# One elementwise product of a graph network's edge layer: VectorE or GpSimd

## The chip, the core and the metric

The kernel runs on one core of a Trainium2 chip. The core has five engines with queues of their own: TensorE (PE, matmul; its weight loads are listed as PEld), VectorE (DVE, elementwise), ScalarE (ACT, functions), GpSimd (POOL) and SyncE (SP, which issues transfers). The transfers themselves run on 16 DMA engines. The metric is the device time of one launch in microseconds (us). Thirteen runs of the kernel before have a median of 5436.42 us and lie between 5418.4 and 5446.99 us.

## The reference

Four graph layers follow each other on 6250 nodes with 128 features and 100000 edges, sorted by their target node. Each layer takes `h = relu(layernorm(x))` and adds its result to `x`. The first averages the neighbours' rows and multiplies by two weight matrices; the third does three such layers; the fourth does three attention layers. The second is the one that matters here, the **product layer**: each edge makes a filter from its weight, and the message that it sends is a product of three vectors and a number, and a node multiplies the messages that arrive.

```python
bf = exp(coeff * (dist[:, None] - centers[None, :]) ** 2)
bf = ssp(bf @ W1 + b1)
bf = ssp(bf @ W2 + b2)
cut = where(dist < R_MAX, 0.5 * (cos(pi * dist / R_MAX) + 1.0), 0.0)
msg = h[src] * edge_feat * bf * cut[:, None]
agg = segment_prod(msg, dst, num_segments=n_nodes)
out = ssp(agg @ W3 + b3)
```

`ssp` is softplus less ln 2, `dist` is the edge weight, `edge_feat` the edge attributes of 128 features.

## The kernel before

The layers run one after the other. In the product layer (`filter_in_order`, from line 846) the edges lie in 128 rows of 784 consecutive edges: partition p holds the edges 784 p to 784 p + 783, the last partition fewer. A column is one edge of each partition. The layer walks the columns in 196 steps of four (`HB`), and its buffers hold eight columns (`NB`). What a step does is spread over six turns of one loop, so that each engine works on another step at the same time; `Pace` and `chain` keep the order in which the loop writes the instructions, on GpSimd for what is handed to `order`, and on PE, DVE and ACT for everything.

For a step i the work is, in this order:

- `inputs(i)`, one turn ahead, in the loop's turn i-1 (line 972): SP loads the edge attributes `ea` (line 883, for eight columns at every second step, in two transfers or three), and GpSimd issues **four gathers** (line 887, recorded at line 67), each of which fetches 128 rows of the node table by the source indices, into four of the eight columns of the tile `rows`. `clocked` (line 888) lets each gather wait for the PE instruction that was written last, the end of `basis` of the same turn. `rows` and `ea` have four buffers each.
- `basis(i)`, turn i: ACT makes the Gaussians `bf` for eight columns at every second step (Square and Exp), and PE makes `z1` with a bias matmul (line 901) and the one with `w1` (line 902).
- `logs(i+2)`, turn i+2: ACT makes the part of the softplus of `z1` that is not linear (Abs, Exp, Ln). The same Exp and Ln serve `z2` of an older step.
- `hidden(i)`, turn i+2: DVE finishes the softplus (`s1`, line 919, shown as s), and PE makes `z2` from a bias (line 921) and four matmuls (line 923).
- **`given(i)`, turn i+3**: the product of the edge attributes with the gathered rows, in place in `ea`, four columns of 128 features at once (line 932, recorded at line 112).
- `factors(i)`, turn i+4: DVE finishes the second softplus (`f2`, line 938, shown as f) and multiplies it by `ea` (line 940).
- `products(i)`, turn i+5: for each column DVE makes `run` (line 957), the running product where the target node is the same as that of the edge before and one where it is not, and multiplies it on (line 959). SP writes the running products `acc` to memory (line 963).

In a turn, `factors(i-4)` and with it the product with `ea` come before `given(i-3)`, so what `given` makes is read one turn later. DVE takes the instructions of `products` between its other ones.

Of the kernel before, what the change touches and what calls it, by code (L numbers as in the profile page):

```python
# [16 lines left out]
OP = mybir.AluOpType  # L17
# [34 lines left out]
def kernel(ctx: ExitStack, tc: tile.TileContext, a: dict, out: bass.AP):  # L52
    nc = tc.nc
# [57 lines left out]
    def tt(o, x, y, op):  # L111
        nc.vector.tensor_tensor(o, x, y, op)  # L112
# [733 lines left out]
    def filter_in_order(table, hist, fl, pool, ps):  # L846
# [9 lines left out]
        order = Pace(0)  # L856
# [69 lines left out]
        def used(i):  # L926
            return 128 if i * HB < L1 else 127

        def given(i):
            h0, n = i * HB % NB, used(i)  # L930
            rows, ea = (x[:n, h0:h0 + HB, :] for x in st["rows", i // 2])
            tt(ea, ea, rows, OP.mult)

        def factors(i, soft):
            h0, n = i * HB % NB, used(i)
# [31 lines left out]
        for i in range(steps + 5):  # L967
            run = products(i - 5) if i >= 5 else iter(())
            if i < steps:
                basis(i)  # L970
            if i < steps - 1:
                inputs(i + 1)
            soft = logs(i) if 2 <= i < steps + 4 else None
            next(run, None)
            if 2 <= i < steps + 2:
                hidden(i - 2, soft)
            next(run, None)
            if 4 <= i < steps + 4:
                for _ in factors(i - 4, soft):
                    next(run, None)  # L980
            next(run, None)
            if 3 <= i < steps + 3:
                given(i - 3)
            for _ in run:
                pass
# [2138 lines left out]
```

## Time and profile before

| what | value |
| --- | --- |
| median of 13 runs | 5436.42 us |
| the profiled execution's own time | 5437.01 us |
| its span, first to last instruction | 5435.2 us |
| busy over the span: PE, DVE, ACT, POOL | 82%, 72%, 61%, 53% |
| gathers of the product layer: count, busy | 784, 804.9 us |
| `ea` times `rows` on DVE: count, median of one | 196, 682 ns |

A group in the profile is a set of instructions of one line, engine, operation and pair of tiles. Its row gives the shapes (partitions x elements), the count, the busy time in us, the mean duration of one in ns, and then the idle time of the engine just before such instructions, with what ended it: "issue" means that nothing in the profile did, "remote" that a semaphore was moved by something that the profile does not tell. An answer for a window counts only what lies in it, in us from the start of the span. The time of a stage is read from its own window, since the shares over the whole span mix layers that are bound by different engines.

### The profile page before, as it was taken

The numbers are of one execution on the slowest core, as the hardware profiler recorded it, in microseconds if no ns is written. First come the engines' busy times: TensorE is split into PE (matmuls) and PEld (weight loads), VectorE is DVE, ScalarE is ACT, GpSimd is POOL, SyncE is SP. The second block draws the span as 40 slices with busy tenths as digits, with TensorE's granted clock in tenths as the row PEclk, the third lists the DMA queues.
The fourth block names the chain that finished last, engine by engine and source line by source line (L and its number), as shares of the span: only waits on it lengthen the run. The fifth ranks groups of instructions, "written<-read, shape, count | busy, mean of one in ns | idle before, by whom it ended". The sixth has DMA issues, their size and how long they took to land. (4 is left out here: it accounts for less than half of the span.)

```text
span 5435.2 us, 83586 instructions
## 1 busy us (share of the span) xinstructions
PE 4478.2 (82%) x25786; PEld 3202.8 (59%) x25786; DVE 3906.1 (72%) x11582; ACT 3315.6 (61%) x6455; POOL 2883.3 (53%) x2871
## 2 busy tenths in 40 slices
PE   1599977787787588899999788889888899788888
PEld 0245533333343255555555677878777788677787
DVE  7998858888888745767687567664666774766664
ACT  5466757777777664433455556667666666656565
POOL 1463047777777536556364366662466662566651
PEclk9999976666656689999999899999999999999999
DMA  4243255555566467888888445443444543444443
GB/s 102 93 170 122 92 173 180 185 184 178 178 185 182 132 181 239 263 252 267 246 268 260 156 128 138 128 132 101 128 129 129 138 134 105 128 126 128 129 128 86
DMA packets 577912, 869.97 MB, mean 160 GB/s; under 512 B 206810, under 2 KB 451991, under 8 KB 569008
## 3 DMA queue, kind: packets, MB, share of 16 engines
q1 hardware_dynamic: 482961, 674.07, 39.7%
q0 software_dynamic: 92160, 188.53, 13.4%
q8 instruction: 205, 3.36, 0.2%
q10 hardware_dynamic: 2332, 1.93, 0.1%
q14 instruction: 254, 2.08, 0.1%
HBM read 565.66 MB, written 298.45 MB: 159 GB/s over the span
## 5 line engine op out<-in xcount | busy, mean ns | idle before, releaser
L67 POOL DMA_INDIRECT rows<-gtable,l_src x1200 | 1195.4, 996 | 795.2 <-issue 291.1
L2604 PE MATMUL cnt<-hot_n,hot_c 128*125 128x250 f32 x3840 | 989.6, 402 | 109.3 <-issue 64.6
L2431 PE MATMUL o<-m,hst 125*128 125x160 f32 x6000 | 954.9, 307 | 102.1 <-issue 99.0
L67 POOL DMA_INDIRECT rows<-table,f_src x784 | 804.9, 1027 | 366.8 <-issue 206.4
L2431 PEld LDWEIGHTS o<-m,hst 125*128 125x128 f32 x6000 | 906.0, 196 | 151.7 <-issue 126.1
L67 POOL DMA_INDIRECT s_rows<-table,s_src x660 | 664.7, 1007 | 419.1 <-issue 174.6
L2604 PEld LDWEIGHTS cnt<-hot_n,hot_c 128*125 128x125 f32 x3840 | 729.3, 199 | 213.1 <-issue 80.8
L2591 ACT ACTIVATE m<-cnt 125x1000 f32<-125x1000 f32 x480 | 478.1, 996 | 449.3 <-remote 213.5
L2422 ACT ACTIVATE hot_c<-hot,coef_t 128x125 f32<-128x125 fp8e4 x1920 | 700.0, 390 | 0.1
L923 PE MATMUL z<-w,s 128*128 128x128 f32 x1568 | 357.0, 399 | 264.4 <-DVE s L121 167.4
L1653 ACT ACTIVATE as_f<-piece 128x1000 fp32r<-128x1000 fp8e4 x390 | 382.1, 1029 | 308.5 <-DMA piece<-adj 99.3
L923 PEld LDWEIGHTS z<-w,s 128*128 128x128 f32 x1568 | 304.3, 289 | 342.5 <-DVE s L121 202.4
L121 DVE SCALAR_TENSOR_TENSOR acc<-acc,ex,rows 125x130 f32<-125x130 f32 x1197 | 424.4, 355 | 35.9 <-issue 0.3
L1544 PE MATMUL o<-as_f,of_two 128*128 128x500 f32 x1560 | 420.1, 414 | 23.0 <-issue 12.0
L1407 ACT ACTIVATE adj<-cnt 128x1000 fp8e4<-128x1000 f32 x250 | 304.2, 1221 | 194.5 <-PE cnt L1406 160.1
L116 DVE TENSOR_SCALAR hot_n<-l_slot,l_id_t 128x250 f32<-128x250 f32 x960 | 301.4, 359 | 167.4 <-remote 88.1
L2421 ACT ACTIVATE hot_n<-half_n 128x250 f32<-128x250 fp8e4 x960 | 384.0, 400 | 18.7 <-issue 10.3
L868 ACT ACTIVATE soft<-z 128x512 f32<-128x512 f32 x392 | 214.6, 585 | 286.4 <-remote 194.4
L1544 PE MATMUL o<-adj,parts 128*128 128x500 fp8e4 x1500 | 359.0, 378 | 0.9 <-ACT adj L1407 0.9
L902 PE MATMUL z<-bf,w 128*128 128x512 f32 x392 | 351.4, 995 | 9.2 <-DMA w_a<-in_L_gnn_W_agg 9.2
L1544 PEld LDWEIGHTS o<-as_f,of_two 128*128 128x128 f32 x1560 | 297.9, 194 | 98.9 <-issue 18.4
L118 DVE TENSOR_SCALAR run<-acc,f_same,f_fresh 128x128 f32<-128x128 f32 (+1 forms) x783 | 298.6, 381 | 19.7 <-DVE acc L121 5.9
(621 smaller groups left out, 7171.8 us busy)
## 6 DMA issues: line engine op xcount, KB each, us to landing
piece<-adj SPq DMA_DIRECT2D x360, 250.0 KB
late_hist<-acc SPq DMA_DIRECT2D x150, 455.0 KB
dist<-ew_dram SPq DMA_DIRECT2D x48, 1024.0 KB
sum_hist<-s_acc SPq DMA_DIRECT2D x132, 320.0 KB
adj<-adj SPq DMA_DIRECT2D x10, 3125.0 KB
hot<-hot SPq DMA_DIRECT2D x240, 128.0 KB
half_n<-node SPq DMA_DIRECT2D x480, 62.5 KB
ea<-in_edge_attr SPq DMA_DIRECT2D x54, 512.0 KB
```

The source lines that it names most:

```text
L67: return nc.gpsimd.indirect_dma_start(out=dst, out_offset=None, in_=table, in_offset=bass.IndirectOffsetOnAxis(ap=idx, axis=0))
L121: nc.vector.scalar_tensor_tensor(o, x, s, y, op0=op0, op1=op1)
L902: nc.tensor.matmul(z1, lhsT=w1, rhs=st["bf"][:, i % 2 * HB:(i % 2 + 1) * HB, :], start=False, stop=True)
L923: nc.tensor.matmul(z2[:, j, :], lhsT=s1[:, j, :], rhs=w2, start=False, stop=j == HB - 1)
L1407: nc.scalar.activation(adj[:, :, NW * (w - w0):NW * (w - w0 + k)].rearrange("p l (w k) -> p w l k", k=NW), cnt[:, :k, :T * NW].rearrange(" ...
L1544: yield nc.tensor.matmul(o[:, :n], lhsT=parts.columns(l, 1, s)[:, 0, :], rhs=adj(l), start=(l == 0 and s == 0), stop=(l == T - 1 and s == ...
L1653: nc.scalar.activation(made[-1], piece[:, at:at + n], AF.Copy)
L2421: nc.scalar.activation(hot_n[:, w, :], half_n[:, w // 2, :], AF.Copy)
L2422: nc.scalar.activation(hot_c[:, w, :P], lt.hot[:, w0 % WB + w, :P], AF.Copy, scale=coef_t[g][:, w0 + w:w0 + w + 1])
L2431: nc.tensor.matmul(o, lhsT=hst[:, l, :D], rhs=m[:P, l, :], start=(l == 0), stop=(l == T - 1))
L2591: nc.scalar.activation(m[:P, :, :, u * 4:u * 4 + 4].rearrange("p l k q -> p k l q"), cnt[:P, :, :T * NW].rearrange("p w (k l) -> p k l w", ...
L2604: nc.tensor.matmul(cnt[:P, w, :T * NW], lhsT=hot_c[:, w, :P], rhs=hot_n[:, w, :], start=True, stop=True)
```

## The change

The product in `given` is handed to GpSimd. It is one instruction on the same tiles, of the same shape and in place as before. It goes through `order.follow`, so that on GpSimd it stands behind the four gathers that `inputs(i + 1)` wrote earlier in the same turn, and ahead of the four gathers of the next turn.

```diff
@@ -929,7 +929,7 @@
         def given(i):
             h0, n = i * HB % NB, used(i)
             rows, ea = (x[:n, h0:h0 + HB, :] for x in st["rows", i // 2])
-            tt(ea, ea, rows, OP.mult)
+            order.follow(nc.gpsimd.tensor_mul(ea, ea, rows))
 
         def factors(i, soft):
             h0, n = i * HB % NB, used(i)
```

## Prediction

> **What bounds the kernel now.** The layers follow each other, so the product layer is a stretch of its own, and what it gains or loses goes into the total. Its bounds come from the first and the last of its gathers (725.4 and 1853.0 us). First view: busy time of the engines in that window. Columns: window, its length, busy us and count of PE, PEld, DVE, ACT, POOL, then granted clock, DMA share and GB/s.
>
> ```profile
> 725.37:1853.03 1127.66, 866.62 (x2334) 426.10 (x2334) 960.72 (x2295) 828.13 (x975) 804.87 (x784) 0.64 0.57 181
> ```
>
> DVE looks like the bound, with 85% (960.72 of 1127.66), and POOL with 71% looks free. That reading would promise a gain. The second view, the groups of 760 to 1850 us, corrects it: look at the idle time behind the bar.
>
> ```profile
> L67 POOL DMA_INDIRECT rows<-table,f_src x758 | 778.8, 1027 | 315.2 <-issue 198.7 <-remote 53.0 <-PE z L902 37.3
> L121 DVE SCALAR_TENSOR_TENSOR s<-z,soft 128x512 f32<-128x512 f32 x190 | 130.2, 685 | 113.5 <-ACT soft L868 97.6 <-issue 13.7 <-PE z L902 1.4
> ```
>
> DVE's idle time has a releaser: `s` waits for ACT's logarithms. Most of POOL's has none. The waits of this window tell in how many pieces, and the timeline shows one turn of it (start, duration, idle before):
>
> ```profile
> POOL rows L67 <- issue: 198.7, 651, 0.6
> ...
> POOL rows L67 <- remote: 53.0, 24, 3.3
> ```
>
> ```profile
> 1204.93 0.94 POOL L67 DMA_INDIRECT rows<-table,f_src  x1 [0.30 <-issue]
> 1206.18 1.14 POOL L67 DMA_INDIRECT rows<-table,f_src  x1 [0.30 <-issue]
> 1207.62 0.94 POOL L67 DMA_INDIRECT rows<-table,f_src  x1 [0.30 <-issue]
> 1208.87 0.95 POOL L67 DMA_INDIRECT rows<-table,f_src  x1 [0.30 <-issue]
> ```
>
> 198.7 us over 651 waits is 0.305 us each: every gather is followed by 0.305 us that nobody ends, so it is part of the gather's price. POOL is then taken for 804.87 + 784 x 0.305 = **1044.0 us of 1127.66**, 5.33 us for each of 196 turns of 5.75. The other 83.7 us are the real waits: 53.0 us in 24 waits (remote) and 37.3 us in 18 (PE's line 902, which `clocked` waits for), each with its 0.305 us inside. In the timeline of PE the bias matmul of line 901 comes at 1201.65, 1206.86 and 1212.05 us, every 5.2 us, with matmuls without a gap between (the granted clock is 0.64 here). So POOL and PE are both near their limit, DVE (5.01 us of work a turn, 981.9 us from 725 to 1875 over 196) is not the one that is last, and the change puts work on the engine with the least room.
>
> **The change, part by part.** *Taken from DVE:* 196 products of 682 ns, 133.7 us.
>
> ```profile
> L112 DVE TENSOR_TENSOR ea<-ea,rows x196: 675/682/693, 735.3 to 1866.9; 128x512 f32<-128x512 f32 x108, 127x512 f32<-127x512 f32 x88
> ```
>
> This is worth nothing on the path as long as a turn takes more than DVE's 5.01 us, which POOL's 5.33 us see to. If that cover were gone, at most 0.68 us a turn would be to gain.
>
> *Put on POOL:* 196 products of 128x512. Of them 191 stand between the first gather and the last (turn 3 brings the first, turn 193 the last that a gather follows); the other five run in the drain, where POOL has no gathers and DVE's turn of over 4 us hides them. POOL computes nothing of this kind in the trace. The nearest rows are those that it writes itself:
>
> ```profile
> L1932 POOL IOTA le_slot<- 128x400 int32 x1 | 0.5, 462 | 0.5 <-issue 0.5
> ...
> L189 POOL IOTA diff<- 128x128 int32 x1 | 0.2, 230 | 0.4 <-POOLq L3113 0.4
> ```
>
> From 128 to 400 elements it takes 232 ns more, 0.853 ns an element, and 121 ns are fixed. One pass over 512 elements is 121 + 437 = 0.56 us: the lower end, since a product writes as much as an IOTA and reads besides. If each of its two reads costs a pass too and nothing overlaps, it is 121 + 3 x 437 = 1.43 us: the upper end. DVE's 0.68 us lies between, but DVE is another engine. Two passes are 0.99 us; I take **1.2 us**, between two and three, because the instruction has two inputs where the IOTA has none.
>
> *Change of work on POOL.* After a gather the trace has a MEMSET start at once (1895.96 us, no idle time), so the 0.305 us is not paid ahead of the product. Behind the MEMSET the next gather waits 1.23 us, behind the IOTA at 2059.51 us 0.63 us, both perhaps for something else. Against the 0.305 us that it replaces, the gap costs from 0 to 0.93 us more; I take 0.3 us, by the IOTA's row. The waits for the gathers and for the two loads of `ea` move from DVE's queue to POOL's. They are for transfers issued four turns before, over 20 us, and the sequencer's waits (17 to 43 ns each) run while the gather ahead is busy: nothing. If a load were late, the next turn's gathers would stand behind the product, and DVE's next `f` times `ea` too.
>
> *Who waits for whom anew.* DVE reads `ea` one turn after the product is written, so its `f2` chain has most of a turn in hand. SP's queue is unchanged: it reloads `ea` when DVE has read it, as before. No transfer is added or moved; the DMA engines are at 0.57.
>
> *POOL's real waits, 83.7 us.* A gather waits for `z1` of its own turn. With POOL's turn at 6.8 us and PE's at 5.2 us, PE has 1.6 us to catch up in each turn, so most of these waits should go. All of them going and all staying are the ends; I keep a quarter, 21 us.
>
> **Sum.** POOL's stretch becomes 1044.0 + 191 x (1.2 + 0.3) + 21 = 1351.5 us against 1127.7 us: **+224 us**. The profiled execution took 5437.01 us around a span of 5435.2 us, 0.6 us over the median of 5436.42 us, so the sum may be set on the median: 5660 us. Ends: 191 x 0.56 = 107 us with no gap and no waits gives +23 us (5460); 191 x (1.43 + 0.93) = 451 us with all waits gives +451 us (5887).
>
> One rule of the Trainium skill speaks against this change: "GPSIMD Engine Reference", section "Elementwise — side-by-side cycle accounting", has a two-input product on GpSimd take 4497 ns for 2048 elements where VectorE takes 2293 ns, and tells to use VectorE for such work. A quarter of 4497 ns is 1.12 us, an estimate from that page; the sum by it would be some 15 us lower than mine. No run here shows that price yet. "SBUF — State Buffer", section "Who interferes with whom", adds that a VectorE instruction with two SBUF inputs and a GpSimd one that reads SBUF block each other for their whole length; the rows of before have no such pair, and the sum by it would be that of the second rival below.
>
> **The rivals.**
> - *A cheap product* (chance 0.13; +25 to +130 us, 5460 to 5565): it runs at 0.56 to 0.68 us without an extra gap. 1044 + 191 x 0.68 = 1174 us, and up to 84 us of waits. For it speaks that POOL starts a MEMSET without a gap and writes at nearly DVE's rate; against it, the two inputs.
> - *POOL and DVE hold each other up* (0.18; over +285 us, 5720 to 5890). In the trace they already do: gathers take 1.14 us instead of 0.95 in some places of each turn, and `run` 0.57 instead of 0.34. If each product first stands behind one of DVE's longer ones, that is 191 x 0.68 = 130 us more: 5790 us. DVE could lose 1.2 us a turn as well and still be under POOL.
> - *Faster* (0.04): the gathers' mean of 1.027 us is above the median of 0.947 us; if DVE, with less to do, leaves them alone and the waits for PE go, 784 x (0.947 + 0.305) + 191 x 0.56 = 1089 us, 39 us less: 5398 us. It decides from a product and gap under (1127.7 - 982) / 191 = 0.76 us with such gathers. With the gathers as they are, it would need 0.44 us, below the lower end.
> - *No change* (0.03): the same halfway, POOL's added work just taking the place of its 83.7 us of waits.
> - That the instruction does not go to GpSimd has no chance worth a number.
>
> **How the numbers follow.** The forecast, POOL sets the turn and the product with its gap costs about 1.2 to 1.8 us, has 0.62 and reaches from 5565 to 5720 us. Slower is 0.62 + 0.18 + 0.13 = 0.93, same 0.03, faster 0.04; 0.2%, 11 us, is about what a measurement of this kernel can tell from no change. The range of 5530 to 5830 us leaves out the no change and faster cases (0.07), the lower part of the cheap one (0.06) and the top of the blocked one (0.05).
>
> **What the profile after would show.** Right: the stretch from the first gather to the last is about 1350 us; a POOL row of `ea` with 196 products of about 1.2 us; a turn of about 6.9 us on POOL without real waits; DVE at 830 us in the window, now waiting for POOL ahead of `f` times `ea`, and PE with gaps. Wrong: products under 0.7 us (cheap), or far over 1.43 us with DVE's two-input rows longer than 683 and 350 ns at the same moments (blocked); waits for PE on POOL that stay at 84 us or grow; or a stretch that is no longer at all.

## The result and the profile after

The changed kernel takes 5601.73 us (median of 8 runs, 5595.95 to 5615.84) against 5433.19 us for the kernel before (median of 37 runs): a ratio of 1.0313, with a 95% interval of 1.03 to 1.0326. That is 168.5 us longer, where the forecast was 224 us.

The profiled execution took 5625.9 us around a span of 5624.0 us, some 24 us over the median. In its trace the stretch from the first gather of the product layer to the last ends is 1292.0 us long instead of 1127.7: 164.3 us more, nearly all of the difference of the medians. Between the last gather and the layer's last instruction on DVE (line 986) lie 5.6 us more; the rest of the trace's difference, 3 us ahead of the layer and 16 us behind it, lies in layers that the change does not touch. The window of the stretch, with the columns as before:

```profile
728.37:2020.32 1291.95, 961.93 (x2333) 457.53 (x2333) 847.00 (x2099) 842.86 (x975) 1075.45 (x975) 0.55 0.48 158
```

DVE has come down from 960.72 to 847.00 us, since its products are gone (131.5 us in the window of before, a part of which overlapped their neighbours), and POOL has gone up from 804.87 to 1075.45 us. The new instruction, and two groups of the page around it:

```profile
L932 POOL TENSOR_TENSOR ea<-ea,rows x196: 1250/1275/1292, 753.1 to 2025.2; 128x512 f32<-128x512 f32 x108, 127x512 f32<-127x512 f32 x88
```

```profile
L67 POOL DMA_INDIRECT rows<-table,f_src x784 | 831.8, 1061 | 257.2 <-issue 236.0
...
L112 DVE TENSOR_TENSOR f<-f,ea 128x512 f32<-128x512 f32 (+1 forms) x196 | 140.4, 716 | 397.0 <-POOL ea L932 397.0
```

The product takes 1.275 us on POOL, 1.87 times DVE's 0.682 us. The waits ahead of the gathers (total, times, longest):

```profile
POOL rows L67 <- issue: 236.0, 676, 44.1
POOL rows L67 <- POOL ea L932: 15.0, 94, 0.2
POOL rows L67 <- DMA rows<-table,f_src: 3.8, 13, 0.3
POOL rows L67 <- remote: 2.4, 1, 2.4
```

The longest, 44.1 us, lies ahead of the first gather and so ahead of the stretch. The rest are the short gaps behind a gather or a product, but for one wait of 2.4 us; before, 53.0 us of "remote" and 37.3 us of waits for PE stood there. DVE's `f` times `ea` waits for POOL in nearly each turn, 397 us in all. One turn in the timeline:

```profile
1304.70 1.28 POOL L932 TENSOR_TENSOR ea<-ea,rows 128x512 f32<-128x512 f32 x1
...
1306.01 0.69 DVE L112 TENSOR_TENSOR f<-f,ea 128x512 f32<-128x512 f32 x1 [2.02 <-POOL ea L932]
1306.14 1.42 POOL L67 DMA_INDIRECT rows<-table,f_src  x1 [0.16 <-POOL ea L932]
...
1307.87 0.94 POOL L67 DMA_INDIRECT rows<-table,f_src  x1 [0.30 <-issue]
...
1309.11 0.94 POOL L67 DMA_INDIRECT rows<-table,f_src  x1 [0.30 <-issue]
...
1310.36 0.95 POOL L67 DMA_INDIRECT rows<-table,f_src  x1 [0.30 <-issue]
1311.33 1.27 POOL L932 TENSOR_TENSOR ea<-ea,rows 128x512 f32<-128x512 f32 x1
```

From product to product it is 6.63 us, and POOL is taken all the time: 1.28 for the product, 0.16, **1.42 for the first gather**, then three gathers of 0.944 with 0.305 between. Three things are to be read from it: the product starts 0.02 us after the gather ahead of it, the next gather follows 0.16 us behind it and not 0.305, and that gather takes half a microsecond more than the other three. The last is new and was not in the sum. Is it the price of changing from one kind of work to another, or something on DVE?

### The profile page after: what moved, and what is told of

Read it like the earlier page. It is cut to its first block, busy times and chain, and to the rows that moved or that the text cites. A ratio compares the mean times of both kernels' runs of the same rounds, so it can differ in the third digit from the quotient of the medians.

```text
span 5624.0 us, 83489 instructions
## 1 busy us (share of the span) xinstructions
PE 4577.4 (81%) x25786; PEld 3233.4 (57%) x25786; DVE 3794.4 (67%) x11386; ACT 3328.3 (59%) x6455; POOL 3154.2 (56%) x3067
## 5 line engine op out<-in xcount | busy, mean ns | idle before, releaser
L67 POOL DMA_INDIRECT rows<-table,f_src x784 | 831.8, 1061 | 257.2 <-issue 236.0
L923 PE MATMUL z<-w,s 128*128 128x128 f32 x1568 | 382.2, 420 | 339.2 <-DVE s L121 339.2
L923 PEld LDWEIGHTS z<-w,s 128*128 128x128 f32 x1568 | 325.8, 307 | 431.0 <-DVE s L121 430.5
L868 ACT ACTIVATE soft<-z 128x512 f32<-128x512 f32 x392 | 229.9, 587 | 444.0 <-issue 371.2
L112 DVE TENSOR_TENSOR f<-f,ea 128x512 f32<-128x512 f32 (+1 forms) x196 | 140.4, 716 | 397.0 <-POOL ea L932 397.0
L902 PE MATMUL z<-bf,w 128*128 128x512 f32 x392 | 398.6, 1120 | 9.0 <-DMA w_a<-in_L_gnn_W_agg 9.0
```

What stands on the lines that cost most here:

```text
L67: return nc.gpsimd.indirect_dma_start(out=dst, out_offset=None, in_=table, in_offset=bass.IndirectOffsetOnAxis(ap=idx, axis=0))
L902: nc.tensor.matmul(z1, lhsT=w1, rhs=st["bf"][:, i % 2 * HB:(i % 2 + 1) * HB, :], start=False, stop=True)
L923: nc.tensor.matmul(z2[:, j, :], lhsT=s1[:, j, :], rhs=w2, start=False, stop=j == HB - 1)
```

## The experiments

The theory is **occupancy**: POOL's own instructions follow each other without a wait and set the turn, what DVE loses is worth nothing, and DVE's waits for POOL are a consequence. The rivals: **hand-over** (DVE gets the product too late and holds up what the gathers wait for), **relief** (DVE's lost work is worth something, which hides a larger cost), and **TensorE** (whose granted clock fell from 0.64 to 0.55 in this stretch). For the long gather: **switch** against **contention** (DVE's `f` times `ea`, which the product's end releases, starts 0.13 us ahead of it).

The runs fell on three chips. On one the kernel before takes 5431 us (the two repeats, nofactor and psum2), on the other two 4867 us (early, tiny, both and none) and 4868 us (copy and the three folds); these two are called the quicker chips here. Each ratio is to the kernel before on the same chip. Some 108 us of the difference between the chips lie in the product layer: its stretch is 1020.1 us in the run tiny, whose time is that of the kernel before, against 1127.7. The times that were expected of early, tiny, both, none and copy were worked out for the chip of 5431 us, so there the ratios, stretches and turns decide.

**after_again and before_again**: the two kernels, unchanged.

> The changed kernel beside the other runs of this call. Occupancy: the stretch of GpSimd is 1292 us on any chip, as in its first profile and in the run with the earlier product, so the difference to the kernel before is 1292 less what that one takes on this chip: 165 us where it waits for TensorE, 270 us where it does not.

> The kernel before, for its trace beside those of this call. Where the chip runs it without the waits for TensorE, GpSimd's stretch from the first gather to the last is 784 x (mean gather + 0.305), about 1020 us, and a turn 5.2 us; where it has them, 1100 us or more.

The changed kernel took 5603.0 us, a ratio of 1.0315 (1.0292 to 1.0337), with a stretch of 1291.8 us. The kernel before took 5437.55 us in one run, with a stretch of 1127.7 us. Both are as in the first traces, to 0.2 us.

**early**: the product one turn earlier on POOL.

```diff
-            if 3 <= i < steps + 3:
-                given(i - 3)
+            if 2 <= i < steps + 2:
+                given(i - 2)
```

> The change, with the product on GpSimd written one turn earlier, so that VectorE reads it two turns later. Occupancy: as the changed kernel, turn 6.6 us, 5590 to 5615 us. Hand-over (VectorE's 2 us of waiting for GpSimd in each turn delay what the gathers wait for): back to about 5440 to 5500 us. Contention: VectorE's product of f2 and ea no longer starts with the first gather, which comes down from 1.42 to 0.95 us; turn 6.15 us, 5500 to 5520 us.

5147.76 against 4866.99 us, a ratio of 1.0578 (1.0558 to 1.0599). The ratio is larger than that of the changed kernel because the kernel before runs its stretch faster on this quicker chip; the stretch itself is 1291.9 us, as in the changed kernel. DVE has been given a turn and still waits as long:

```profile
  DVE f L112: 393.6, 193
```

This line of the answer on the product's line lists who waited for it: 393.6 us in 193 waits. Hand-over falls: DVE runs ahead until it meets POOL's latest product, wherever that stands in the program. The first gather stayed at 1.42 us, since DVE's product is still released by POOL's, so this run does not tell switch from contention.

**nofactor**: the changed kernel without DVE's `f` times `ea` (the messages then lack the edge attributes and the rows).

```diff
-            tt(f2, f2, ea[:, h0:h0 + HB, :], OP.mult)
+            pass
```

> The changed kernel without VectorE's product of f2 and ea (left out); the product on GpSimd stays. Contention (the gather behind the product is held by this product on VectorE until it ends): that gather comes down from 1.42 to 0.95 us, the turn from 6.63 to 6.16 us, about 90 us less than the changed kernel. Switch (the gather is long because of the work of another kind before it): it stays at 1.42 us, and the time within 10 us of the changed kernel.

5510.42 us, a ratio of 1.0146 (1.0124 to 1.0168), so 93 us less than the changed kernel on the same chip; the stretch is 1213.9 us. The gather behind the product:

```profile
1299.86 1.27 POOL L932 TENSOR_TENSOR ea<-ea,rows 128x512 f32<-128x512 f32 x1
1301.29 0.99 POOL L67 DMA_INDIRECT rows<-table,f_src  x1 [0.16 <-POOL ea L932]
```

From 1.42 to 0.99 us: of the 0.48 us, 0.43 were contention and 0.04 stay. These 0.04 us may be the switch's: in the run both below, where nothing runs on DVE when that gather starts, it takes 0.99 us as well. In the changed kernel 190 of the 191 long gathers start while that product runs on DVE.

**tiny**: one element a partition written by POOL behind the gathers, DVE's product kept.

```diff
-            tt(ea, ea, rows, OP.mult)
+            tt(ea, ea, rows, OP.mult); order.follow(nc.gpsimd.memset(spare[:, 0, 0:1], 0.0))
```

> The kernel before, and behind the four gathers of a turn GpSimd writes one element a partition into a spare tile (about 0.1 us). Switch (work of another kind between two gathers costs by itself: in the changed kernel the gather behind the product takes 1.42 us instead of 0.944, less 0.145 us of shorter gaps): 0.33 + 0.1 us a turn, up to 83 us, less what comes out of the 84 us of waits: 5440 to 5520 us, and a first gather of 1.4 us in its place in the turn. Contention (the 0.47 us come from VectorE's product of f2 and ea, which the product on GpSimd releases at that moment): no more than 0.1 us a turn, 5430 to 5450 us, and the first gather as long as the others.

4869.91 against 4866.99 us, a ratio of 1.0002 (0.9991 to 1.0013). The gather behind the memset takes 0.95 us, the one ahead of it 1.15:

```profile
1304.84 1.15 POOL L67 DMA_INDIRECT rows<-table,f_src  x1 [0.30 <-issue]
1305.99 0.11 POOL L932 MEMSET spare<- 128x1 f32 x1
1306.29 0.94 POOL L67 DMA_INDIRECT rows<-table,f_src  x1 [0.19 <-issue]
```

0.11 and 0.19 us take the place of the 0.305 us between two gathers, to the hundredth. A switch to an instruction as small as this costs nothing. The long gather stands where DVE's products are: 195 of the 784 take over 1 us, and 194 of these start while one of DVE's two products runs.

**both**: DVE's product kept, and a product of `rows` with itself on POOL.

```diff
-            tt(ea, ea, rows, OP.mult)
+            tt(ea, ea, rows, OP.mult); order.follow(nc.gpsimd.tensor_mul(spare[:n], rows, rows))
```

> VectorE keeps its product, and GpSimd makes one more of the same shape into a spare tile, where the change has it. Occupancy (GpSimd's own instructions set the turn; VectorE's relief is worth nothing): the turn is that of the changed kernel, 6.6 us, and the time 5590 to 5640 us. Relief (the change would cost more, but VectorE's 0.68 us a turn are given back): longer than the changed kernel by up to 196 x 0.68 = 133 us, 5660 to 5735 us.

5095.95 us, a ratio of 1.0469 (1.045 to 1.0488), and a stretch of 1244.2 us. It does not decide as it was meant to: the product of a tile with itself takes 1.051 us and not 1.276, so the turn is 6.37 us instead of 6.63, and the time is under that of the run early on the same chip (5147.76 us), although DVE does more. The shorter product accounts for most of that, so relief is spoken against but not ruled out by this run alone. What it shows besides is a DVE instruction that is held:

```profile
1306.05 1.75 DVE L121 SCALAR_TENSOR_TENSOR acc<-f,cut,run 128x128 f32<-128x128 f32 x1
1306.59 1.06 POOL L932 TENSOR_TENSOR spare<-rows 128x512 f32<-128x512 f32 x1
```

`acc` takes 0.35 us elsewhere. Here one of each turn's four (190 in all) takes over 1.5 us and ends 0.16 us behind POOL's product. Its record begins 0.54 us ahead of that product; what held it until then is open.

**none**: the product left out on both engines.

```diff
-            tt(ea, ea, rows, OP.mult)
+            pass
```

> The product with the gathered rows is left out on both engines; the gathers stay. Occupancy: VectorE was not the one that is last, so 5420 to 5445 us. Relief: gathers that VectorE no longer holds up come down to 0.947 us and the waits for TensorE go, 784 x 1.252 = 982 us instead of 1128: down to 5290 us.

4857.9 us, a ratio of 0.9981 (0.9968 to 0.9993): 9 us less, less than the 133.7 us of DVE's products by far. POOL's stretch is 1024.7 us, although DVE is done with the layer 105 us before its end:

```profile
713.40:1632.98 919.58, 743.56 (x2353) 378.54 (x2353) 869.39 (x2156) 836.52 (x984) 706.58 (x700) 0.75 0.67 217
1632.98:1738.14 105.16, 0.48 (x1) 0.18 (x1) 0.00 (x1) 0.00 (x0) 79.56 (x85) 0.50 0.20 57
```

In the second window only POOL works, on the last 85 gathers. On this chip, then, the gathers set the stretch already before the change. tiny, which keeps DVE's product, agrees: its gathers' 781.4 us and 784 x 0.305 us are its whole stretch. DVE is not far behind there, with 976.7 us busy of 1020.1.

**copy**: as tiny, with a copy of 128x512 on POOL, one input in place of two.

```diff
+            tt(ea, ea, rows, OP.mult); order.follow(nc.gpsimd.tensor_copy(spare[:n], rows))
```

> The kernel before, and behind the four gathers of a turn GpSimd copies the four columns of rows into a spare tile, an instruction with one input in place of two. Passes (each input costs one, as the sum of the prediction bounds it): 0.6 to 1.0 us instead of 1.275, the sum on GpSimd 982 to 1044 + 191 x (0.5 to 0.85) = 1077 to 1206 us against the 1128 us of the kernel before, so 5430 to 5515 us. If the inputs do not matter: 1.27 us, and 5560 to 5600 us.

4935.77 us, a ratio of 1.0147 (1.0124 to 1.017), which is 68 us; the copy takes 0.615 us, near one pass by the IOTA's rows (0.56). Two inputs cost more: 1.05 us with the same tile twice (both), 1.275 with two tiles. Why the last two differ was not tried.

**psum2**: the kernel before, with the two products of DVE made by way of PSUM, so that neither has two inputs in SBUF.

```diff
-            stt(f2, st.pop(("z2", i))[:n], 0.0, soft[:n, Z1:]...., OP.max, OP.add)
+            stt(z2, z2, 0.0, soft[:n, Z1:]...., OP.max, OP.add)
             yield
-            tt(f2, f2, ea[:, h0:h0 + HB, :], OP.mult)
+            tt(z2, z2, st["rows", i // 2][0][:n, h0:h0 + HB, :], OP.mult); tt(f2, z2, ea[:, h0:h0 + HB, :], OP.mult)
```

> The kernel before with the same products on VectorE in another place: the softplus of z2 is finished in place in PSUM, multiplied by the rows there, and then by ea into f2, so that no VectorE instruction of 512 elements has two inputs in SBUF. Contention: no gather is held, all take 0.945 us, GpSimd's turn is 4 x 1.25 = 5.0 us instead of 5.2 to 5.3, and the time is 20 to 60 us under the kernel before. Rival (gathers are slowed by the two-port form of run, or TensorE at 5.2 us a turn is the bound): no change, within 10 us.

5436.27 us, a ratio of 1.001 (0.9996 to 1.0025). Half of the expectation held. The gathers:

```profile
L67 POOL DMA_INDIRECT rows<-table,f_src x784 | 742.2, 947 | 429.4 <-issue 250.6 <-PE z L901 45.7 <-PE z L923 38.5
```

None is held by the products now: 0.947 us in the mean instead of 1.027, 62.7 us less in all, and the longest takes 1.065 us. But the stretch is 1127.6 us, as before to 0.1 us: POOL's idle time grew by just these 62.6 us (from 366.8 to 429.4), and the waits in it for PE grew from 39.4 to 103.4 us. So on this chip the holding was hidden in the kernel before, and POOL alone was not what set its stretch. One thing is left open: PE was busy for longer in this run (906.2 us instead of 866.6, at a granted clock of 0.61 instead of 0.64), and whether the edit itself slowed PE was not tried.

**fold, foldpsum, foldafter**: the bias matmul of `z1` taken out, 0.6 us of PE a turn, in the kernel before, in psum2 and in the changed kernel. The bias goes into ACT's Abs, DVE's max and the bias of `z2`.

```diff
-            nc.tensor.matmul(z1, lhsT=b1, rhs=ones_b...., start=True, stop=False)
-            nc.tensor.matmul(z1, lhsT=w1, rhs=st["bf"]...., start=False, stop=True)
+            nc.tensor.matmul(z1, lhsT=w1, rhs=st["bf"]...., start=True, stop=True)
...
-                act(soft[:, :Z1], z1.rearrange("f c q -> f (c q)"), AF.Abs)
+                act(soft[:, :Z1], z1.rearrange("f c q -> f (c q)"), AF.Abs, bias=fl.b1c)
...
-            stt(s1, st.pop(("z1", i)), 0.0, soft[:, :Z1]...., OP.max, OP.add)
+            stt(s1, st.pop(("z1", i)), fl.b1n, soft[:, :Z1]...., OP.max, OP.add)
```

> The kernel before without the bias matmul of z1 (0.6 us of TensorE a turn): the bias goes into ScalarE's Abs, VectorE's max and the bias of z2, which costs no instruction a turn. TensorE (its pace, and not GpSimd's 5.3 us or VectorE's 5.0 us, sets the turn of 5.75 us in the kernel before): its waits on GpSimd go, the stretch comes from 1128 down to the sum of the gathers, 1044 to 1060 us, the time 70 to 84 us under the kernel before. GpSimd or VectorE: no change, within 10 us.

> The same, and VectorE's products by way of PSUM, so that no gather is held. TensorE and then GpSimd: the two limits are relieved together, the stretch comes down to 784 x 1.252 = 982 us, at most 1020 us, and the time is 110 to 146 us under the kernel before, where the second edit alone brought nothing. If GpSimd is not the next limit: as the run before.

> The changed kernel without the bias matmul of z1. Occupancy of GpSimd: TensorE has 1.4 us a turn to spare there, so no change, within 10 us of the changed kernel, and a stretch of 1292 us. TensorE (its clock, 0.55 in this stretch, and not GpSimd sets the turn of 6.63 us): up to 0.6 x 196 = 118 us less.

They ran on the third chip, a quicker one. fold: 4885.26 against 4868.11 us, a ratio of 1.0034 (1.0019 to 1.0049); foldpsum: 4905.86 us, 1.0086 (1.0064 to 1.0108); foldafter: 5155.42 us, 1.0592 (1.0567 to 1.0617). foldafter does what occupancy says: its stretch is 1290.4 us, 1.6 us less than the changed kernel's, with the 116.4 us of bias matmuls gone and the clock at 0.61 instead of 0.55; so the lower clock is no cause. fold and foldpsum brought nothing, and DVE's `s` went from 0.683 to 0.745 us with the bias as its scalar. On this chip PE was not last, so there were no long waits for it to take away; on the chip where they are, the two were not run. foldpsum failed in its second half too: its gathers take 745.2 us instead of fold's 792.5, yet its stretch is 1032.7 us and not at most 1020, with waits for PE and DVE in place of what the gathers gave up. This fits a kernel before in which POOL, DVE and PE lie close together, so that freeing one brings little; which of them holds foldpsum was not tried. No version here that computes the layer beats the kernel before.

## Why the prediction was right, and where its sizes were off

The mechanism held in each step that decides. POOL sets the turn after the change (no wait for PE left; early and foldafter do not move it). DVE's 133.7 us were worth nothing that shows (none: 9 us on one chip). The time, 5601.7 us, is within the range, 58 us under the forecast. The stretch, term by term:

| term | forecast | measured |
| --- | --- | --- |
| gathers with their 0.305 us | 1044.0 | 979 unheld (784 x 1.249) + 90 held (191 x 0.47) |
| 191 products | 229 (1.2 us) | 244 (1.276 us) |
| change of work | +57 (0.3 us) | -24 (0.02 + 0.16 - 0.305 us) |
| real waits (PE, remote) | 21 | 2 |
| sum | 1351.5 | 1291 (trace: 1292.0) |

**The step that was mis-sized is the change of work.** I took 0.3 us more from the IOTA's row; its 0.63 us of idle time were a wait for PE, as the row's own releaser says. The MEMSET's 1.23 us were probably for something else too, since tiny has 0.19 us behind one. tiny shows that a small instruction fits into the 0.305 us between two gathers. The term is 81 us too high, the products and gathers together 40 us too low and the waits 19 us too high, which leaves the 60 us by which the sum missed the trace.

**The gathers were right by luck.** 1044 us was the sum with DVE's holding in it. In the changed kernel three gathers of four are free of it and the fourth is held longer, because POOL's product itself releases DVE's, just ahead of the gather. The second rival named this contention but looked for it in the wrong place: in the turns of the stretch the product itself is not held, the gather behind it is.

**The drain (what follows the last gather) was put at nothing and cost 5.6 us.** The prediction had DVE's turn hide the five products behind the last gather. POOL makes them in one go, and DVE's `f` times `ea`, which the first of them releases, then takes 5.39 us instead of 0.69, and ends 0.55 us behind the last one:

```profile
2020.33 6.15 POOL L932 TENSOR_TENSOR ea<-ea,rows 127x512 f32<-127x512 f32 x5
2021.64 5.39 DVE L112 TENSOR_TENSOR f<-f,ea 127x512 f32<-127x512 f32 x1 [2.01 <-POOL ea L932]
```

Here POOL's products do hold DVE, as the second rival feared for every turn. In the turns of the stretch they don't, because DVE is waiting for the product while it runs.

**"Most of a turn in hand" for DVE was misread.** DVE waits 2.0 us for POOL in each turn. When one engine sets the pace, what reads its results runs up to the newest of them, and shows as waiting; the run early gave a turn more and changed nothing.

**What the kernel before is bound by** was half right. POOL had the least room, so work put on it had to show. But the turn of 5.75 us is a mean: half of the turns take up to 5.4 us, and 53 of 195 over 5.8. In the stretch of before, ACT stands still 31 times ahead of its work on `z`, until a signal whose sender the profile does not tell:

```profile
ACT soft L868 <- remote: 192.1, 31, 10.7
```

tiny, on a quicker chip, has no such wait. And psum2 took 62.7 us from POOL's instructions and none from the stretch: there it is POOL's waits for PE that end last. What makes PE late on that chip, and not on the others, stays open; fold might have told it and fell on a quicker chip. It also sets the size of the effect: the changed stretch is 1290 to 1292 us on all three, and the cost is what is left of it above the old one, 168 us where that is 1128 us, and 281 us (early against its kernel before) where it is about 1020 us. The changed kernel itself was run only on chips of the first kind.

## What to carry to other kernels

Work moved to an engine with a low busy share is not free when that engine's idle time has no releaser: count the gap that follows each of its instructions as part of them first. The moved products are 250 us long; they cost 281 us (in early) where that engine had no real waits to give up, and 168 us where it had 84 us of them. An instruction that releases another engine's two-input work just ahead of the next gather adds to that gather, so look at what starts when a moved instruction ends. A wait of a consumer in each turn says which engine is last, not that the hand-over is late.

## What the runs showed of the hardware

- A gather that starts while a DVE product of 128x512 with two inputs in SBUF runs is held: 1.42 us where that product had 0.57 us to go, 0.944 us without it. With one of the inputs in PSUM (psum2) none is held, and the largest of 784 took 1.065 us; in the changed kernel, 190 gathers start while `s` runs, which has the same shape and one input in PSUM, and take 0.944 us. The Trainium skill, "SBUF — State Buffer", section "Who interferes with whom", has such a product contend with GpSimd's reads, but names `tensor_tensor` among the operations that did not stall DMAs issued from GpSimd; these runs show that it holds a gather, for most of what is left of it (0.48 of 0.57 us). Which part of the gather waits is not shown.
- The same section has a VectorE instruction with two SBUF inputs blocked for the whole length of a GpSimd instruction that reads SBUF. The drain of the changed kernel agrees, with `f` times `ea` at 5.39 us instead of 0.69 beside POOL's products, and so does both, where `acc` ends 0.16 us behind POOL's product and takes 1.75 us instead of 0.35.
- An elementwise instruction on GpSimd of 128x512 in 32 bits took 0.615 us with one input, 1.051 us with one tile as both inputs and 1.276 us with two. "GPSIMD Engine Reference", section "Elementwise — side-by-side cycle accounting", gives 4497 ns for an add of two inputs of 2048 elements; a quarter of that, 1.12 us, is an estimate from the page for the product here (the prediction took the row for a product), and the measured price is 14% above.
